# Four lanes sorted by expert and four dense, instead of five and three, with other planner costs, in a two-layer decoder

## The chip, the cores and the metric

The kernel runs on one core of one Trainium2 chip. The metric is the device time of one execution in microseconds. A run gives one such time; where a profile is shown, it is of one execution, and its span is the time from the first to the last instruction of the program.

## The reference, cut to what matters

The input `x` is 16 sequences of 128 tokens with 256 features, in float32. Two decoder layers are applied to it; every line of the sketch below adds its result to `x`, after a layer norm.

```python
x = x + attn0(ln(x))              # one head, causal, q k^T through one 256x256 matrix
x = x + xattn0(ln(x), ctx, mask)  # 16 heads of 16, keys and values from ctx
x = x + ffn0(ln(x))               # 16 blocks of 64, each token takes the best 4 by a router
x = x + attn1(ln(x))              # 16 heads of 16, own residual inside
x = x + xattn1(ln(x), ctx, cell)  # windows of 64, rotary, masked by cell, norms with gains
x = x + moe1(ln(x))               # 8 experts of 128 (SwiGLU), best 2 of a sigmoid router,
                                  # weights normalised and times 2.5, plus a shared expert of 256
```

The change is in how `moe1` is computed for some of the sequences, and in the order of everything.

## The kernel before

**Lanes and layers.** Two sequences form a lane (256 tokens), so there are eight lanes, 0 to 7. A lane's `x` stays in SBUF as a tile of 128 partitions by 2 by 256. Each lane goes through `layer_0` (causal attention, attention to the context, block FFN) and `layer_1` (self-attention, windowed attention to the context, and then the experts).

**Two ways through the experts.** A *dense* lane runs `expert_ffn` (L1272): all eight experts and the shared one are computed for all of its tokens (`gu` is gate and up, ten tiles of four matmuls; `y` is down, with 20 matmuls over two sequences), and a matmul with the router's weights (`wb`) scales each expert's `hm`. A *sorted* lane belongs to a group (`GROUPS`, L34). `routing` (L981) ranks the experts, counts the rows of each and scatters each token's normalised row into the DRAM buffer `to_experts`, four indirect DMAs of 128 rows for a lane. When the last lane of the group has been routed, `sorted_experts` (L1338) runs `plan` (L1075), which works out for each tile of 128 rows which expert it belongs to, and then all its `expert_tile`s (L1118): a gather of the expert's weights (`we<-in_L_experts`), a gather of the rows (`we<-to_experts`), two transposes (`xgt`), `gu<-we`, a transpose `hT`, `y<-we`, and a store to the DRAM buffer `by_experts`. A group of n lanes has 2 x n x 256 / 128 + 7 tiles, 27 for five lanes. The shared expert of a sorted lane runs by itself (`shared`, L1040). Then `combining` (L1168) gathers the results of each lane (`yg`, four gathers) and adds them to `x` with the token's weights, and the lane is written out. All indirect DMAs are issued from POOL's queue; loads, stores of `x`, and the swaps of the rotary step go through SP's queue; the stores to `by_experts` through ACT's.

**The order is made by a planner at build time.** The class `Turns` (L82) runs the lanes as threads. A thread says which engine it wants next and which buffers it takes; `run` (L229) picks the thread with the smallest key and records its next piece, so that the order on each engine's queue is fixed when the kernel is built. The planner has a clock of its own: `charge` adds a cost to an engine, `HOP` and `HOP_FROM_PE` stand for the way from one engine to another, `SWITCH` for a change of TensorE's array shape, `PART` for a piece on TensorE, `RELEASE` for the time until a buffer that was given back can be taken, `indexed` (L162) for an indirect DMA and its landing. `LIMITS` (L385) says how many buffers there are of each kind. `first` marks a thread in the midst of an attention's scores; the planner lets it go `LEAD` ns ahead of others. These numbers issue nothing; they only move the order.

**Lanes in flight.** `more` (L1447) starts the next (layer, lane) pair of `TURN` when fewer than `IN_FLIGHT` of them are under way (L1441). The dense `expert_ffn` of lanes that are not in a group starts when its weights (`late_weights`, L1408) have been loaded, one lane after another.

Of the kernel before, what the change touches and what calls it, by code (L numbers as in the profile page):

```python
# [30 lines left out]
BPC = P // 64  # L31
NE, TOPE = 8, 2

GROUPS = ((0, 1, 2, 3, 4),)  # L34


OUT = -(2.0**100)
# [44 lines left out]
class Turns:  # L82
# [3 lines left out]

    LEAD = 100.0
    HOP = 70.0  # L90
    HOP_FROM_PE = 200.0
    SWITCH = 91.0
    PART = 20.0
    RELEASE = 30.0

    def __init__(self, nc, limits):
        self.nc = nc
# [19 lines left out]
    def give(self, tag, n=1):  # L117
        self.tiles[tag] += [self.now.at + self.RELEASE] * n

    def shaped(self, shape):  # L120

        if shape != self.shape:
            self.shape = shape
            self.charge(PE, self.SWITCH)

# [36 lines left out]
    def indexed(self, out, out_index, src, src_index):  # L162

        at = lambda i: None if i is None else bass.IndirectOffsetOnAxis(ap=i, axis=0)
        self.charge(POOL, 1050.0)
        self.moved(4 * int(np.prod((src if src_index is None else out).shape)))
        self.now.at += 2000.0
        self.nc.gpsimd.indirect_dma_start(out, at(out_index), src, at(src_index))  # L168

    def fetch(self, out, src):  # L170
# [58 lines left out]
    def run(self, more):  # L229

        while True:
            more()
            best = None
            for i, th in enumerate(self.threads):
                if th.ask is None:
                    continue
                engine, takes = th.ask
                at = self.reach(th, engine)
                ok = True
                for tag, n in takes.items():  # L240
                    left = sorted(self.tiles[tag])
                    if not n:
                        continue
                    if len(left) < n:
                        ok = False
                        break
                    at = max(at, left[n - 1])
                first = th.holds or "s" in takes
                tiled = engine == PE and self.shape != WHOLE and ("s" in takes or "oT" in takes)
                key = (max(at - self.LEAD * first, self.free_at[engine] - first), not first, not tiled, th.rank, i)  # L250
                if ok and (best is None or key < best[0]):
                    best = key, th, at
            if best is None:
                assert not self.threads, "no thread can go on"
                return
            _, th, at = best
            engine, takes = th.ask
            for tag, n in takes.items():
                self.tiles[tag].sort()
                del self.tiles[tag][:n]  # L260
            th.at, th.last = max(th.at, at), engine
            if engine == PE:
                self.free_at[PE] += self.PART
            self.resume(th, None)
# [10 lines left out]
def decoder(ctx: ExitStack, tc: tile.TileContext, a: dict, out: bass.AP):  # L275
# [31 lines left out]
    first = wts.tile([P, 4, DC, D], F32, tag="f3", name="first")  # L307
# [51 lines left out]
    class Sorted:  # L359
# [16 lines left out]

    groups = [Sorted(k, lanes) for k, lanes in enumerate(GROUPS)]
    group_of = {l: g for g in groups for l in g.lanes}
# [4 lines left out]


    LIMITS = dict(  # L385
        bank=4, s=2, oT=1, xn=5, xT=4, qk=5, qs=3, kb=3, v=3, p=6, oS=2, on=4, xe=3, hm=5, tmp=3,
        rank=2, selT=2, p0=2, pT0=2, unseen=4, chosen=3, swap=1, words=1, top=3,
    )
    q = Turns(nc, LIMITS)

    def new(tag, shape, name, dtype=F32):
        return work.tile(shape, dtype, tag=tag, name=name, bufs=LIMITS[tag])
# [682 lines left out]
    def plan(g):  # L1075


        yield DVE, dict(tmp=3)
        T, E1 = g.tiles, NE - 1
        n_full = g.cap // P  # L1080
        little = lambda name, n: small.tile([P, n], F32, tag=name, name=name, bufs=1)
        n = little("n_of", NE)
        q.dve("tensor_tensor", n, g.next_row, g.first_row, ALU.subtract)
        q.dve("tensor_scalar", n, n, 1.0 / P, None, ALU.mult)
        t = new("tmp", [P, NE, n_full], "n_full")
        full = consts[:, C_IOTA : C_IOTA + n_full].unsqueeze(1).to_broadcast([P, NE, n_full])
        q.dve("tensor_tensor", t, along(n, n_full), full, ALU.is_gt)
        tiles = little("tiles", NE)
        q.dve("tensor_reduce", tiles, t, AX.X, ALU.add)
        tri = consts[:, C_TRI8 : C_TRI8 + NE * NE].rearrange("p (e f) -> p e f", f=NE)  # L1090
        t = small.tile([P, NE, NE], F32, tag="n_tri", name="n_tri", bufs=1)
        q.dve("tensor_tensor", t, tri, tiles.unsqueeze(1).to_broadcast([P, NE, NE]), ALU.mult)
        first = little("first", NE)
        q.dve("tensor_reduce", first, t, AX.X, ALU.add)
        q.dve("scalar_tensor_tensor", g.offset, first, float(P), g.first_row, ALU.mult, ALU.subtract)
        end = little("end", NE)
        q.dve("tensor_tensor", end, first, tiles, ALU.add)
        iota = consts[:, C_IOTA : C_IOTA + T]
        each = lambda v: v[:, 0:E1].unsqueeze(1).to_broadcast([P, T, E1])
        past = new("tmp", [P, T, E1], "past")  # L1100
        q.dve("tensor_tensor", past, along(iota, E1), each(end), ALU.is_ge)
        e = little("e_of", T)
        q.dve("tensor_reduce", e, past, AX.X, ALU.add)
        t = new("tmp", [P, T, E1], "t_of")
        q.dve("tensor_tensor", t, past, each(tiles), ALU.mult)
        f = little("f_of", T)
        q.dve("tensor_reduce", f, t, AX.X, ALU.add)
        q.dve("tensor_tensor", f, iota, f, ALU.subtract)
        q.dve("tensor_scalar", f, f, float(P), float(g.cap - P), ALU.mult, ALU.min)
        q.dve("scalar_tensor_tensor", f, e, float(g.cap), f, ALU.mult, ALU.add)  # L1110
        for to, v in ((g.tile_rows, f), (g.tile_weights, e)):
            if v is e:
                q.dve("tensor_scalar", v, v, float(P), None, ALU.mult)
            q.dve("tensor_scalar", v, v, consts[:, C_ROW : C_ROW + 1], None, ALU.add)
            q.dve("tensor_copy", to, v)
        q.give("tmp", 3)

    def expert_tile(g, i):  # L1118

        yield POOL, dict(p=1)  # L1120

        we = new("p", [P, HC, S], "we").rearrange("p h s -> p (h s)")
        xg = yo = we[:, 3 * D :]
        q.indexed(we[:, 0 : 3 * D], None, a["L1_experts"], g.tile_weights[:, i : i + 1])
        yield POOL
        q.indexed(xg, None, g.to_experts, g.tile_rows[:, i : i + 1])
        yield PE, dict(bank=1)
        t = bank([P, DC, S], "xgt")
        for d in range(DC):
            q.transpose(t[:, d, :], xg[:, d * P : (d + 1) * P], ident)  # L1130
        yield ACT, dict(xe=1)
        xgT = new("xe", [P, DC, S], "xgT")
        q.act("copy", xgT, t)
        q.give("bank")
        yield PE, dict(bank=1, tmp=1)
        gu = bank([P, 2, P], "gu2")
        for d in range(DC):
            wt = we[:, d * D : (d + 1) * D].rearrange("p (n f) -> p n f", f=P)
            q.matmul(gu, xgT[:, d, :], wt, start=d == 0, stop=d == DC - 1)
        q.give("xe")  # L1140
        yield ACT
        sg = new("tmp", [P, P], "sg2")
        q.act("activation", sg, gu[:, 0, :], AF.Tanh, scale=0.5)
        yield DVE, dict(p0=1)
        h = new("p0", [P, P], "h2")
        q.dve("scalar_tensor_tensor", sg, sg, 1.0, gu[:, 0, :], ALU.add, ALU.mult)
        q.dve("scalar_tensor_tensor", h, sg, 0.5, gu[:, 1, :], ALU.mult, ALU.mult)
        q.give("tmp")
        q.give("bank")
        yield PE, dict(bank=1)  # L1150
        t = bank([P, P], "hT2")
        q.transpose(t, h, ident)
        q.give("p0")
        yield ACT, dict(pT0=1)
        hT = new("pT0", [P, P], "hT")
        q.act("copy", hT, t)
        q.give("bank")
        yield PE, dict(bank=1)
        y = bank([P, D], "y2")
        q.matmul(y, hT, we[:, DC * D : 3 * D], start=True, stop=True)  # L1160
        q.give("pT0")
        yield ACT
        q.act("copy", yo, y)
        q.give("bank")
        q.load(g.by_experts[i * P : (i + 1) * P, :], yo, engine=ACT)
        q.give("p")
# [170 lines left out]

    def sorted_experts(g):  # L1338
        yield from plan(g)
        yield [expert_tile(g, i) for i in range(g.tiles)]  # L1340
        part_ended(g)

# [95 lines left out]
            if g.left == 0:  # L1438
                q.start(sorted_experts(g), 2 * NL + min(g.lanes), at)

    IN_FLIGHT = 6  # L1441

    TURN = [(0, l) for l in range(6)]
    for l in range(NL):
# [2 lines left out]
    def more():  # L1447
        n = begun[0]
        if n < IN_FLIGHT and n not in arrives:
            return  # L1450
# [123 lines left out]
```

## Time and profile before

| | us |
|---|---|
| median of three runs | 845.04 |
| lowest and highest | 844.15, 847.82 |
| the profiled execution | 846.62 |
| its span, first to last instruction | 844.8 |
| PE busy | 775.1 (92%), 7902 matmul records |
| DVE busy | 474.6 (56%) |
| ACT busy | 393.0 (47%) |
| POOL busy | 445.4 (53%) |
| PE's share of the chain that ended last | 72% |
| mean granted TensorE clock | 0.969 |

PE is TensorE's matmuls and PEld its weight loads, which lie beside them; DVE is VectorE, ACT ScalarE, POOL GpSimd, SP the queue of SyncE. A float32 matmul that is not a transpose leaves two records. Matmuls are pipelined, so their durations overlap, and the time that one costs is read from the distance between starts. In names of tiles the buffer numbers are left out. A line is mostly that of a helper (L135 the matmuls, L140 the transposes, L144 DVE, L149 ACT, L155 POOL, L168 the indirect DMAs), so groups are told apart by their tiles.

### The profile page before, as it was taken

How to read it: one execution, taken by the hardware profiler on the slowest of the kernel's cores; microseconds unless marked ns; L12 is line 12 of the kernel's file. 1: busy time of each engine (PE TensorE's matmuls, PEld its weight loads, DVE VectorE, ACT ScalarE, POOL GpSimd, SP SyncE). 2: the span in 40 equal slices, each digit the busy share in tenths (PEclk: the TensorE clock that was granted, in tenths of full speed). 3: DMA queues.
4: the chain of work that ended last, by engine and by line, in shares of the span. 5: the costliest groups of instructions: out<-in, count | busy, mean ns of one | idle time of the engine just before them, and what ended most of it. 6: DMA issues, size and time to landing. Idle time of an engine off the chain costs nothing.

```text
span 844.8 us, 19702 instructions
## 1 busy us (share of the span) xinstructions
PE 775.1 (92%) x7902; PEld 610.1 (72%) x7902; DVE 474.6 (56%) x1201; ACT 393.0 (47%) x874; POOL 445.4 (53%) x688
## 2 busy tenths in 40 slices
PE   6999999999999999999999899989894899988848
PEld 5877777887787876777687677757673577866726
DVE  5455746536654375827817768685667435245533
ACT  4545652533635565555465666547442344233100
POOL 5345654433533474728954678676646735450530
PEclk9999999999999999999999999989897899999969
DMA  9356642231110120001014111110205334551330
GB/s 306 99 158 191 192 118 69 80 103 26 28 38 24 34 77 2 28 26 51 13 65 151 46 45 45 45 38 33 64 33 150 113 101 137 156 181 48 103 94 25
DMA packets 60938, 70.43 MB, mean 83 GB/s; under 512 B 8848, under 2 KB 52496, under 8 KB 60208
## 3 DMA queue, kind: packets, MB, share of 16 engines
q1 hardware_dynamic: 51584, 46.24, 17.7%
q0 software_dynamic: 5376, 19.40, 7.7%
q10 hardware_dynamic: 3888, 3.54, 1.2%
q8 instruction: 62, 1.02, 0.5%
q14 instruction: 28, 0.23, 0.1%
HBM read 43.99 MB, written 20.97 MB: 77 GB/s over the span
## 4 chain that ended last, share of the span: by engine, by line
PE 72%; DVE 10%; POOL 7%; issue 4%; ACT 3%; DMA 2%; another core or an unknown queue 1%; SPq 0%; ACTq 0%; POOLq 0%; DVEq 0%
PE s L135 14%; PE pj L135 11%; PE y L135 9%; PE gu L135 9%; PE pr L135 8%; PE hp L135 7%; PE oT L135 4%; PE tps L140 3%; PE o L140 2%; DVE top L144 2%; POOL rstd L155 2%; POOL we L168 1%; ACT p L149 1%; POOL kb L155 1%
## 5 line engine op out<-in xcount | busy, mean ns | idle before, releaser
L144 DVE TENSOR_REDUCE top<-s 128x8 f32<-128x1024 f32 x96 | 112.8, 1217 | 49.6 <-PE s L135 49.0
L149 ACT ACTIVATE p<-s 128x1024 f32<-128x1024 f32 x96 | 93.2, 1022 | 48.6 <-PE s L135 45.4
L155 POOL TENSOR_TENSOR qs<-qT,less 128x512 f32<-128x512 f32 x48 | 61.4, 1281 | 58.0 <-ACT less L149 57.1
L155 POOL TENSOR_SCALAR rstd<-mv 128x2 f32<-128x2 f32 x77 | 18.6, 242 | 105.2 <-DVE mv L144 97.5
L149 ACT ACTIVATE sg<-gu 128x256 f32<-128x256 f32 (+1 forms) x67 | 22.2, 340 | 98.5 <-PE gu L135 56.3
L135 PE MATMUL hp<-srcT,L_w 128*128 128x256 f32 x256 | 65.2, 384 | 0.0
L135 PE MATMUL s<-kb,qT 32*128 32x256 f32 x768 | 61.2, 407 | 4.0 <-DVE top L144 2.6
L135 PE MATMUL s<-qs,kb 32*128 32x128 f32 x1536 | 58.8, 283 | 4.2 <-DVE top L144 1.4
L135 PEld LDWEIGHTS s<-qs,kb 32*128 32x128 f32 x1536 | 48.9, 186 | 18.1 <-issue 9.3
L155 POOL TENSOR_TENSOR rstd<-rstd,power 128x2 f32<-128x2 f32 x77 | 55.8, 724 | 6.4
L155 POOL TENSOR_SCALAR kb<-kT,consts 128x256 f32<-128x256 f32 x96 | 54.8, 582 | 4.6 <-ACT kT L149 3.6
L135 PE MATMUL y<-L_w,hm 128*128 128x256 f32 x256 | 57.0, 381 | 0.0
L135 PE MATMUL gu<-srcT,gu 128*128 128x256 f32 x192 | 50.4, 414 | 6.2 <-issue 2.6
L135 PE MATMUL oT<-p,v 128*32 128x128 f32 x1536 | 53.3, 278 | 1.3 <-ACT oS L149 0.7
L144 DVE TENSOR_TENSOR x<-x,y 128x512 f32<-128x512 f32 x16 | 11.0, 684 | 76.7 <-PE y L135 76.7
L135 PEld LDWEIGHTS s<-kb,qT 32*128 32x128 f32 x768 | 38.0, 186 | 21.5 <-issue 7.9
L135 PEld LDWEIGHTS y<-L_w,hm 128*128 128x128 f32 x256 | 48.2, 190 | 7.0 <-issue 0.5
L135 PEld LDWEIGHTS hp<-srcT,L_w 128*128 128x128 f32 x256 | 44.5, 191 | 9.8 <-issue 1.7
L135 PEld LDWEIGHTS gu<-srcT,gu 128*128 128x128 f32 x192 | 38.2, 207 | 16.4 <-issue 3.1
L144 DVE SCALAR_TENSOR_TENSOR sg<-sg,gu 128x256 f32<-128x256 f32 (+1 forms) x67 | 24.4, 364 | 44.9 <-ACT sg L149 41.6
L168 POOL DMA_INDIRECT we<-in_L_experts,tile_weights x27 | 26.4, 978 | 43.5 <-ACT hT L149 7.6
L135 PEld LDWEIGHTS oT<-p,v 128*32 128x32 f32 x1536 | 40.0, 111 | 12.9 <-issue 8.9
(216 smaller groups left out, 1791.3 us busy)
## 6 DMA issues: line engine op xcount, KB each, us to landing
to_experts<-zero SPq DMA_DIRECT2D x7, 1280.0 KB
unseen<-hidden SPq DMA_DIRECT2D x128, 64.0 KB
c<-in_ctx SPq DMA_DIRECT2D x16, 256.0 KB
by_experts<-we ACTq DMA_DIRECT2D x27, 128.0 KB
x<-in_x SPq DMA_DIRECT2D x8, 256.0 KB
L_w<-in_L_w SPq DMA_DIRECT2D x2, 1024.0 KB
hidden<-plain SPq DMA_DIRECT2D x32, 64.0 KB
swap<-kT SPq DMA_DIRECT2D x16, 128.0 KB
```

The source lines that it names most:

```text
L135: self.nc.tensor.matmul(out, lhsT, rhs, **kw)
L140: self.nc.tensor.transpose(out, src, ident)
L144: getattr(self.nc.vector, name)(out, *args, **kw)
L149: getattr(self.nc.scalar, name)(out, *args, **kw)
L155: getattr(self.nc.gpsimd, name)(out, *args, **kw)
L168: self.nc.gpsimd.indirect_dma_start(out, at(out_index), src, at(src_index))
```

## The change

The group has lanes 0 to 3, and lane 4 becomes dense; 27 expert tiles become 23, 20 scatters and 20 gathers of results become 16 each. In the planner, `LEAD` goes away and a thread in an attention is preferred only among equals, `SWITCH` is larger, `RELEASE` is zero, an indirect DMA lands 1.5 us later, and the expert tiles begin 3 us after the plan. There is one `xn` buffer more and one `qs` buffer less, and five (layer, lane) pairs are in flight instead of six.

```diff
-GROUPS = ((0, 1, 2, 3, 4),)
+GROUPS = ((0, 1, 2, 3),)
...
-    LEAD = 100.0
     HOP = 70.0
     HOP_FROM_PE = 200.0
-    SWITCH = 91.0
+    SWITCH = 115.0
     PART = 20.0
-    RELEASE = 30.0
+    RELEASE = 0.0
...
         self.moved(4 * int(np.prod((src if src_index is None else out).shape)))
-        self.now.at += 2000.0
+        self.now.at += 3500.0
         self.nc.gpsimd.indirect_dma_start(out, at(out_index), src, at(src_index))
...
-                first = th.holds or "s" in takes
                 tiled = engine == PE and self.shape != WHOLE and ("s" in takes or "oT" in takes)
-                key = (max(at - self.LEAD * first, self.free_at[engine] - first), not first, not tiled, th.rank, i)
+                key = (at, not (th.holds or "s" in takes), not tiled, th.rank, i)
...
-        bank=4, s=2, oT=1, xn=5, xT=4, qk=5, qs=3, kb=3, v=3, p=6, oS=2, on=4, xe=3, hm=5, tmp=3,
+        bank=4, s=2, oT=1, xn=6, xT=4, qk=5, qs=2, kb=3, v=3, p=6, oS=2, on=4, xe=3, hm=5, tmp=3,
...
     def sorted_experts(g):
         yield from plan(g)
+        q.now.at += 3000.0
         yield [expert_tile(g, i) for i in range(g.tiles)]
         part_ended(g)
...
-    IN_FLIGHT = 6
+    IN_FLIGHT = 5
```

## The prediction

> **What bounds the kernel now.** I read the table of windows first, then the timelines of the engines in the two windows that stand out. In the table each row is a stretch of the span (its bounds and length in us), the busy time of PE, PEld, DVE, ACT and POOL with the number of instructions, the granted TensorE clock, the DMA share and GB/s.
>
> ```profile
> 300.00:575.00 275.00, 260.29 (x3290) 200.06 (x3288) 181.84 (x435) 156.30 (x315) 185.36 (x289) 0.98 0.14 46
> 575.00:625.00 50.00, 45.41 (x553) 34.73 (x541) 34.72 (x91) 25.91 (x56) 29.47 (x46) 0.93 0.14 44
> 625.00:675.00 50.00, 34.95 (x323) 24.95 (x316) 26.26 (x71) 17.66 (x44) 33.51 (x45) 0.83 0.41 119
> 675.00:737.00 62.00, 59.85 (x429) 48.88 (x428) 25.75 (x78) 26.34 (x74) 29.90 (x37) 1.00 0.45 135
> 800.00:825.00 25.00, 11.78 (x37) 8.73 (x38) 10.60 (x27) 2.02 (x6) 9.05 (x10) 0.73 0.32 98
> ```
>
> TensorE sets the time: it is busy 92% of the span, and in 675:737, where a dense lane and expert tiles run together, it is idle 2.15 us of 62. It has two holes: 625:675 (idle 15.05 us, clock 0.83) and 800:825 (idle 13.22 us, clock 0.73). The change pays TensorE work for a chance to fill these two.
>
> In the first hole only lanes 6 and 7 are still in attention, no dense lane has begun, and lane 7's keys and queries have to be rotated and spread on POOL. POOL's timeline (start, length, instruction, idle before and its releaser):
>
> ```profile
> 633.11 1.28 POOL L155 TENSOR_TENSOR qT<-qT,consts 128x512 f32<-128x512 f32 x1 [3.49 <-DMA swap<-qT]
> 639.83 1.03 POOL L168 DMA_INDIRECT we<-in_L_experts,tile_weights  x1 [5.44 <-DVE on L144]
> 643.38 1.27 POOL L155 TENSOR_TENSOR qT<-qT,swap 128x512 f32<-128x512 f32 x1
> 652.75 1.28 POOL L155 TENSOR_TENSOR kT<-kT,consts 128x512 f32<-128x512 f32 x1
> 656.87 2.17 POOL L155 TENSOR_SCALAR kb<-kT,consts 128x256 f32<-128x256 f32 x4
> ```
>
> The first gather of weights waits 5.44 us, and the second half of qT's rotation stands behind it and two more; eight gathers (0.95 us and 0.30 between) lie between 639.83 and kT's first product at 652.75. TensorE meanwhile has only the first expert tiles.
>
> The second hole lies at the burst of 20 gathers (`yg`, 786.9 to 811.8, one every 1.25 us) that fetch the sorted lanes' results. ACT, DVE, POOL and PE in that place:
>
> ```profile
> 801.78 0.38 ACT L149 ACTIVATE sg<-gu 128x256 f32<-128x256 f32 x1 [15.16 <-remote]
> 815.08 0.94 ACT L149 ACTIVATE sg<-gu 128x256 f32<-128x256 f32 x3 [12.92 <-remote]
> 815.11 0.42 DVE L144 TENSOR_TENSOR hm<-wb,hm 128x256 f32<-128x256 f32 x1 [11.65 <-remote]
> 810.84 0.95 POOL L168 DMA_INDIRECT yg<-by_experts,results  x1 [0.30 <-issue]
> 815.59 0.37 PE L135 MATMUL wb<-selT,experts 128*128 128x256 bf16 x1 [10.47 <-DVE hm L144]
> ```
>
> The last dense lane's `gu` matmuls had been issued by 805.1, yet ACT and DVE get on only at 815.1, 3.3 us after the burst's last issue ended (811.79). What holds them is not named ("remote"); that it ends with the burst is what I build on. Then TensorE runs at half clock (0.50 in 815:820, 0.60 in 820:825).
>
> **Part 1: one lane goes from sorted to dense (+14.7 us of TensorE work).** Spacing in the last dense lane, where nothing waits:
>
> ```profile
> 826.43 1.89 PE L135 MATMUL gu<-srcT,gu 128*128 128x256 f32 x8
> 828.16 0.27 PE L135 MATMUL wb<-selT,experts 128*128 128x256 bf16 x1
> 828.27 1.89 PE L135 MATMUL gu<-srcT,L_shared 128*128 128x256 f32 x8
> 831.95 3.62 PE L135 MATMUL y<-down,hm 128*128 128x256 f32 x16
> 835.40 1.03 PE L135 MATMUL y<-L_shared,hm 128*128 128x256 f32 x4
> ```
>
> From start to start, eight `gu` take 1.73 us, one `wb` 0.11, sixteen `y` 3.45. A dense lane adds 8 experts x 1.73 = 13.8, 32 `y<-down` = 6.9, 8 `wb` = 0.9 and two `ptt` = 0.1: 21.7 us. The shared expert and the router are in both paths. The sorted path loses four expert tiles (27 become 23), each 0.86 for `gu<-we`, 0.22 for `xgt`, 0.11 for `hT`, 0.43 for `y<-we` by the spacing at 741 to 744: 6.5; and four transposes and five rank counts, 0.6. Net 21.7 - 7.1 = +14.6; two more changes of array shape in the order (333 to 335) at 0.09 each (eight `pj` take 1.73 or 1.82) make it +14.7. All of it is on the path, since TensorE is the bound.
>
> The other engines: DVE gets 8 `hm<-wb`, 8 `hm<-sg` and 8 `sg` at 0.42 and loses 4 x (2 x 0.29 + 0.48) plus small ones, about +6 us. ACT gains 8 x 0.38 and loses 4 x (0.37 + 0.37 + 0.27 + 0.27): -2 us. POOL loses 8 weight and token gathers, 4 scatters and 4 result gathers, 16 x 1.25 = 20 us. DVE is at 56% and hidden by TensorE; were it not, its 6 us would add.
>
> **Part 2: the first hole (-14 us).** In the new order the first weight gathers stand ahead of lane 6's last attention instead of in lane 7's rotation, and lane 4, now dense, has its `gu` between lane 7's swap of kT and the first scores that need it: 17.7 us of TensorE work there by the spacings above, against 7.0 before. The path it must cover is the swap's DMA (2.72), 1.28, 0.68, 1.27 and 2.17 for `kb`: 8.1 us. So 7.0 did not cover, and 17.7 covers it with some gathers in front. I let the stage become like its neighbour 575:625, idle 4.6 of 50: -10.5. A clock of 0.83 is 17 us at half, 0.93 is 7 us; ten us less at half, busy 70% of it, save another 3.5. Together -14.0. Bounds: -19 (all of the idle and 4 us of clock) and -2 (POOL queues as before; lane 7 late again).
>
> **Part 3: the burst (-7 us).** Sixteen gathers instead of 20 end it 4 x 1.25 = 5.0 us earlier, and a dense lane is again the work beside it: `gu` of four tiles, then blocked banks. Half of the 3.9 us that the slow clock cost on 7.8 busy us of 815:825 may go: -2. Behind it there is now a whole further dense lane, so nothing of the sorted path can end last. Bounds: 0 (same stall) and -16 (no stall).
>
> The Trainium skill, "TensorE: Matmul & The Clock Gate", the two states, speaks against the -2: the clock falls to half after an idle window of about 3.4 us, and a stall of 10.5 - 5.0 = 5.5 us is still longer. By it the term would be -5 and the time 840.7; the trace agrees in that 10.47 us of idle was followed by 0.50. The skill's "SBUF — State Buffer", who interferes with whom, says that a DMA never contends with a compute engine, which speaks against the burst as the cause; by it Part 3 is 0 and the time 845.7. The 15.16 and 12.92 us of ACT beside the burst decide against that page for me, but nothing here shows the mechanism.
>
> **Part 4: the planner's costs and limits (0, between -8 and +17).** LEAD, RELEASE, SWITCH and the later landing of gathers issue nothing; they move the order everywhere. The landing was 3.07 us for `yg` (794.41 to 797.48), so a longer assumption puts consumers further behind, which costs nothing where a dense lane fills. A third `qs` buffer less can hold back POOL's 1.28 us `qs`; it is written and read within one attention, and `xn` gets one more: 0. The 3 us from the plan keep the first gather from standing in POOL's queue with normalisations behind it: the 5.44 us above, already in Part 2. Five lanes in flight instead of six is the risk, priced below.
>
> **Sum.** 844.8 + 14.7 - 14.0 - 7.0 + 0 = 838.5 of span. The profiled execution is 846.6, 1.8 more than its span, and 1.6 above the median of 845.0; so 838.5 + 1.8 - 1.6 = **838.7 us**. A measurement of this kernel can tell about 0.5% (4.2 us) from no change: faster is below 840.8, slower above 849.3.
>
> **Rivals.**
> - **Five lanes starve the middle (slower).** With six lanes TensorE idles 14.7 us of 275 (5.3%) in 300:575; with two lanes left, 15.05 of 50 (30%). Straight between them, one lane fewer costs 6.2% of 275 = +17 us: 855.7. It makes the change slower from +10.6 us on. For it: DVE and POOL are at two thirds in that stretch, so waits are already near. Against: TensorE is busy 94.7% there, so six lanes are more than enough in most of it, and a straight line overstates the loss of one. Chance 0.2.
> - **The first hole is not filled.** POOL's queue delays lane 7 as before, Part 2 gives -2 and Part 3 -3: 844.8 + 14.7 - 5 = 854.5, so 854.7. Chance 0.15.
> - **Half of the gain.** Parts 2 and 3 bring 10 to 18 together: 841 to 849. Chance 0.2.
> - **Both holes go.** -19 and -14: 826.5, so 826.7. For it: three dense lanes stand behind the sorted tiles. Chance 0.13.
>
> **How the numbers follow.** The forecast (830 to 840.8) has 0.32, and with both holes gone (below 830) 0.45 are faster, 0.2 the same, 0.35 slower. 825 to 858 leaves out about a tenth at each end; the forecast's own range is 830 to 841.
>
> **What would show it.** Right: 256 records of `gu<-srcT,gu` and 128 of `y<-down`, no window of 50 us between 550 and 700 with TensorE below 43, and a stall beside `yg` of 4 to 7 us. Wrong: idle in 300:575 above 25 us (five lanes); a hole with `kb` late on POOL; a stall at `yg` as long as before with 16 gathers, or none, which would take the burst's length out as its measure.

## Result: 1.1% slower, and the profile after

The changed kernel takes 854.36 us (median of four runs, 853.54 to 856.78) where the kernel before took 845.34 beside it (844.15 to 847.82): a ratio of 1.0108, 95% interval 1.0076 to 1.0139. The forecast of 838.7 has the wrong sign. The profiled execution has a span of 855.0 us against 844.8, and the mean granted clock rose from 0.969 to 0.982.

The table of windows of the changed kernel (columns as before: bounds, length, busy time of PE, PEld, DVE, ACT, POOL, granted clock, DMA share, GB/s):

```profile
300.00:575.00 275.00, 259.81 (x3133) 200.04 (x3125) 180.14 (x421) 151.75 (x313) 179.01 (x278) 0.99 0.14 46
575.00:625.00 50.00, 39.89 (x598) 28.41 (x598) 34.97 (x82) 26.40 (x50) 27.95 (x41) 0.95 0.12 39
625.00:675.00 50.00, 42.33 (x284) 33.29 (x288) 29.29 (x81) 21.49 (x58) 27.68 (x41) 0.91 0.34 106
675.00:737.00 62.00, 57.32 (x566) 44.57 (x567) 26.97 (x74) 26.94 (x69) 33.79 (x46) 1.00 0.34 107
...
800.00:855.00 55.00, 49.31 (x223) 40.97 (x223) 25.17 (x64) 6.67 (x18) 1.38 (x2) 0.96 0.09 30
```

The deep hole of before (34.95 busy of 50 in 625:675) is now spread: 39.89 and 42.33 in two neighbours that together were 80.36 and are 82.22. The stretch from 800 on is full but for its first us and the 3.9 us behind TensorE's end. And 300:575 looks the same, 259.81 against 260.29. By busy time alone one would say that the change gained. Busy time misleads here, because a matmul that follows its neighbour late, or runs at half clock, is busy too.

So I split TensorE's time in another way, my own working from the starts of its records. Each record is given the distance it keeps to its neighbour where nothing waits at full clock (0.216 us for a float32 matmul of 256 columns, as in Part 1, and so on for each kind). Their sum is TensorE's **own work**. What its span up to its last record has beyond that is **lost**: idle, half clock, late neighbours. The last column is the time from TensorE's end to the end of the span.

| | own work | lost in the first 400 us of own work | lost from 400 to 600 | lost in the rest | behind TensorE | span |
|---|---|---|---|---|---|---|
| before | 709.3 | 38.4 | 60.4 | 32.8 | 4.1 | 844.8 |
| after | 724.0 | 52.9 | 52.9 | 21.4 | 3.9 | 855.0 |

The work grew by 14.7 us, exactly what Part 1 says. The end became better by 11.4, the middle by 7.5, and the first part became worse by 14.5. The first part ends at about 440 us before and 457 after; the first sorted lanes have scattered their rows by then (from 375 and 377 us on), but no gather and no expert tile of the group has begun. For that last figure the prediction had only its Part 4, at 0.

At the burst, ACT, PE and POOL of the changed kernel (start, length, instruction, idle before and releaser):

```profile
799.18 0.38 ACT L148 ACTIVATE sg<-gu 128x256 f32<-128x256 f32 x1 [7.39 <-remote]
804.12 0.66 ACT L148 ACTIVATE sg<-gu 128x256 f32<-128x256 f32 x2 [4.55 <-remote]
800.53 3.78 PE L134 MATMUL gu<-srcT,gu 128*128 128x256 f32 x8 [6.17 <-DVE sg L143]
804.63 1.99 PE L134 MATMUL gu<-srcT,gu 128*128 128x256 f32 x8 [0.32 <-DVE hm L143]
800.54 1.15 POOL L167 DMA_INDIRECT yg<-by_experts,results  x1 [0.30 <-issue]
```

TensorE's stall is 6.17 us where it was 10.47, and the eight `gu` after it take 3.78 us where the next eight take 1.99: half clock, as before (the granted clock is 0.56 in 800:805 and 1.00 behind it). Behind the stall a whole dense lane follows with almost nothing lost. The Trainium skill, "TensorE: Matmul & The Clock Gate" (what's actually happening), puts the fall to half clock after about 3.4 us of idle; 6.17 us followed by half speed agrees with it.

### The profile page after: what moved, and what is told of

Its sections match the earlier page's. It is cut to its first block, busy times and chain, and to the rows that moved or that the text cites. A ratio compares the mean times of both kernels' runs of the same rounds, so it can differ in the third digit from the quotient of the medians.

```text
span 855.0 us, 19810 instructions
## 1 busy us (share of the span) xinstructions
PE 790.5 (92%) x7963; PEld 621.8 (73%) x7963; DVE 482.3 (56%) x1201; ACT 391.8 (46%) x865; POOL 427.3 (50%) x668
## 4 chain that ended last, share of the span: by engine, by line
PE 74%; DVE 14%; ACT 4%; issue 3%; POOL 2%; another core or an unknown queue 1%; DMA 1%; POOLq 0%; DVEq 0%; ACTq 0%
PE s L134 14%; PE y L134 12%; PE gu L134 11%; PE pj L134 10%; PE pr L134 8%; PE hp L134 6%; DVE top L143 4%; PE oT L134 4%; PE tps L139 2%; ACT p L148 2%; PE o L139 2%; DVE xn L143 1%; POOL rstd L154 1%; DVE st L143 1%
## 5 line engine op out<-in xcount | busy, mean ns | idle before, releaser
L148 ACT ACTIVATE sg<-gu 128x256 f32<-128x256 f32 (+1 forms) x71 | 24.6, 349 | 105.3 <-PE gu L134 85.2
L134 PE MATMUL gu<-srcT,gu 128*128 128x256 f32 x256 | 63.7, 400 | 8.1 <-DVE sg L143 6.2
L134 PE MATMUL s<-kb,qT 32*128 32x256 f32 x768 | 63.6, 407 | 4.8 <-ACT p L148 3.6
L134 PEld LDWEIGHTS s<-qs,kb 32*128 32x128 f32 x1536 | 48.6, 186 | 19.9 <-issue 10.0
L134 PEld LDWEIGHTS gu<-srcT,gu 128*128 128x128 f32 x256 | 49.0, 199 | 18.7 <-DVE sg L143 6.4
L154 POOL TENSOR_TENSOR rstd<-rstd,power 128x2 f32<-128x2 f32 x76 | 55.3, 727 | 6.3
L154 POOL TENSOR_SCALAR kb<-kT,consts 128x256 f32<-128x256 f32 x96 | 52.7, 560 | 3.6 <-ACT kT L148 2.8
L148 ACT ACTIVATE hm<-hp,cols 128x256 f32<-128x256 f32 x64 | 26.8, 470 | 45.3 <-PE hp L134 44.8
L148 ACT COPY oS<-oT 128x512 f32<-128x512 f32 x48 | 28.3, 590 | 39.1 <-PE oT L134 35.7
```

Of the source, the lines that this page charges most:

```text
L134: self.nc.tensor.matmul(out, lhsT, rhs, **kw)
L148: getattr(self.nc.scalar, name)(out, *args, **kw)
L154: getattr(self.nc.gpsimd, name)(out, *args, **kw)
```

## Experiments

Eighteen kernels ran. In the code, "before" and "after" name the kernel that was edited. Ratios are to the kernel before, run beside it on the same chip; its medians there were 845.9 to 848.2. Where two kernels did not run side by side, the text gives the difference of their ratios and that of their medians, since the kernel before itself moves by up to 2.9 us from one set of runs to another.

### The group, and the lanes in flight

**g4_six**: before with the group of four. With RELEASE at 20 as well, since the planner finds no order otherwise.

```diff
-GROUPS = ((0, 1, 2, 3, 4),)
+GROUPS = ((0, 1, 2, 3),)
-    RELEASE = 30.0
+    RELEASE = 20.0
```

> The kernel before with lanes 0 to 3 sorted and lane 4 dense, and nothing else of the change: six pairs in flight, the planner's costs as before but RELEASE 20 for 30 (30 gives no order that can be built with four lanes). Theory 'five in flight' (the 16 us that TensorE loses more up to the end of layer 0 come from five lanes instead of six, and four sorted lanes by themselves gain): 845 + 14.7 of work - about 20 of idle after layer 0 = 840, and TensorE's lost time up to the last block FFN stays near 38 us as before. Rival 'the dense lane' (the extra work is what is lost, the rest comes out even): 855 to 860. Rival 'every new order' (the order of a planner scatters by that much whatever is changed): anything from 840 to 865, with lost time up to the last block FFN anywhere from 38 to 55.

867.87 us, ratio 1.0225 (1.0174 to 1.0276).

**before_release20**: the same RELEASE alone, the control.

> The kernel before with RELEASE 20 for 30 and nothing else, a number that issues nothing and moves the order from TensorE's 285th row on. It is the partner of the run with lanes 0 to 3 sorted, six in flight and RELEASE 20. Theory 'every new order' (the order before is a picked one, and any other loses ten us and more): 855 to 870, TensorE's lost time up to the last block FFN 45 or more where before has 38. Rival 'four sorted lanes do it' (with six in flight the dense lane disturbs the middle): 845 to 849, lost time near 38.

849.14, ratio 1.0036 (1.0007 to 1.0065). The control costs 2 to 3 us, so the group of four with six in flight costs 16 to 17: its 14.7 of work, and 66.1 us lost in the first 400 of own work where the control loses 42.1, against gains behind it.

**g5_five**: before with five in flight (LEAD is 90 because 100 gave no order).

```diff
-    LEAD = 100.0
+    LEAD = 90.0
-    IN_FLIGHT = 6
+    IN_FLIGHT = 5
```

> The kernel before with five pairs in flight instead of six and LEAD 90 for 100 (100 gives no order that can be built), still five lanes sorted. Theory 'five in flight': 845 + 16 = 861, the loss lying ahead of the last block FFN. Rival 'the dense lane': 845, within 3. Rival 'every new order': 840 to 865.

879.75, ratio 1.0372 (1.0355 to 1.0389). It loses 63.9 us in the first 400 of own work. Taken by itself this is the rival of the five lanes, nearly twice as dear as I had priced it; what LEAD 90 has in it was not run alone.

**g4_five**: both, and nothing else of the change.

```diff
-GROUPS = ((0, 1, 2, 3, 4),)
+GROUPS = ((0, 1, 2, 3),)
-    IN_FLIGHT = 6
+    IN_FLIGHT = 5
```

> The kernel before with two parts of the change: a group of four lanes and five lanes in flight; the planner's settings as before. Theory 'the group of four pays for itself only where the planner leaves the sorted lanes' end uncovered or the early order poor': the group of five with five in flight lost 164.7 us on TensorE (879.4 of span); work rises by 14.7, and with three dense lanes as cover the losses of 16.7 at the end go: 870 to 885. Rival 'five in flight needs the fourth dense lane, and the two belong together' (as after's settings suggest): 850 to 862, near after's 854.

845.71, ratio 0.9977 (0.9957 to 0.9996). Both of my expectations were wrong. Each part alone, with the nudge of RELEASE or LEAD that it needed, costs 16 to 32 us, and together they cost nothing: 32.3 us lost in the first 400 of own work, less than before's 38.4. So neither five lanes nor the group has a price of its own there; what has one is the order that the planner finds for them. This run is also the base for all that follows: the same own work as the changed kernel (724.0) and the same five lanes in flight, in 9 to 11 us less.

**after_g5**: the changed kernel with the group of five.

```diff
-GROUPS = ((0, 1, 2, 3),)
+GROUPS = ((0, 1, 2, 3, 4),)
```

> The changed kernel with five lanes sorted again and everything else of the change kept. Theory 'five in flight': 854.4 - 14.7 of work + about 20 that the dense lane fills after layer 0 = 860. Rival 'the dense lane': 845 or less. Rival 'every new order': 840 to 865.

873.88, ratio 1.0296 (1.0272 to 1.032). Less work by 14.7 and yet 16 to 20 us slower than the changed kernel, which none of the three expected; 25.9 us lie behind TensorE's end, where the changed kernel has 3.9. TensorE's last matmuls and POOL's last gather:

```profile
847.80 1.03 PE L134 MATMUL y<-L_shared,hm 128*128 128x256 f32 x4
860.19 0.95 POOL L167 DMA_INDIRECT yg<-by_experts,results  x1 [0.30 <-issue]
```

The dense lanes are done while the sorted lanes' results are still being gathered. The group of four pays here because one more dense lane covers that end.

**after_six** and **after_six_then_five**: the changed kernel with six in flight (SWITCH is 95, as 115 gave no order), and with six for the first ten starts only.

```diff
-    IN_FLIGHT = 5
+    IN_FLIGHT = 6
```

> The changed kernel with six pairs in flight instead of five and SWITCH 95 for 115 (115 gives no order that can be built). Theory 'five in flight': 854.4 - 16 = 838, with TensorE's lost time up to the last block FFN back near 38 us. Rival 'the dense lane': 854, within 3. Rival 'every new order': 840 to 865, and the lost time ahead of the last block FFN does not go with the number in flight.

> The changed kernel with six pairs in flight for the first ten starts and five from then on. Theory 'five in flight': the lost time up to the last block FFN falls from 54 to about 40 and the rest stays, 840 to 845. Rival 'every new order': 855 to 870.

862.32 (1.0155, 1.0123 to 1.0187) and 869.43 (1.0257, 1.0236 to 1.0278): the theory of the five lanes had expected 838 and 840 to 845, and is refuted by both. With six throughout, the first 400 us of own work lose 44.8 in place of 52.9, and the rest gives back more (91.4 in place of 74.3); with six for the first ten, the first part loses 63.6. But SWITCH differs in the first of them, so the next run belongs beside it.

**after_switch100**: the changed kernel with SWITCH 100 in place of 115.

> The changed kernel with SWITCH 100 for 115, which issues nothing and moves the order from TensorE's 676th row on. Theory 'every new order': 862 to 875, that is, the changed kernel's order is a picked one too. Rival 'the number in flight sets the middle': 854, within 3, and lost time up to the last block FFN within 3 us of the changed kernel's 54.

862.33, ratio 1.0149 (1.0089 to 1.0208; 855.11 to 865.75). Against the changed kernel's 1.0108 (1.0076 to 1.0139) that is 3 to 8 us more, by ratios or by medians, and the intervals overlap. A number that issues nothing and leaves the work alone does as much as six lanes with SWITCH 95. So the difference of after_six cannot be put down to the lanes.

### The landing part

**before_landing**: before with the two edits that make gathers land later in the planner.

```diff
-        self.now.at += 2000.0
+        self.now.at += 3500.0
         self.nc.gpsimd.indirect_dma_start(out, at(out_index), src, at(src_index))
...
         yield from plan(g)
+        q.now.at += 3000.0
```

> The kernel before with the gather part of the change alone: an indirect DMA lands 1.5 us later in the planner and the tiles begin 3 us after the plan. The order is the same up to TensorE's row 1636 of 3130. If the distance from the plan helps the hole behind the plan, TensorE loses 5 to 10 us less between the first gather of weights and the first dense gu, 836 to 842. If any new order costs, 850 to 865, with the loss in the part that is reordered only.

854.72, ratio 1.0081 (1.0061 to 1.0101). TensorE itself loses 116.8 us, 14.7 less than before, but its last matmul ends at 826.0 and the sorted lanes go on for 27.7 us. So the time lies where 'any new order' had put it, but the loss does not: TensorE gained, and the end was left uncovered. The ends of PE, of POOL's gathers and of DVE's combine:

```profile
825.03 1.03 PE L135 MATMUL y<-L_shared,hm 128*128 128x256 f32 x4
844.24 0.95 POOL L168 DMA_INDIRECT yg<-by_experts,results  x1 [0.30 <-issue]
847.23 0.48 DVE L144 SCALAR_TENSOR_TENSOR x<-yg,weight,x 128x256 f32<-128x256 f32 x1 [0.41 <-DMA yg<-by_experts,results]
```

**landing_held_lane**: the same, and the last dense lane starts only when all expert tiles are done, to cover that end.

```diff
-        if ready and experts_begun[0] < len(dense):
+        if ready and experts_begun[0] < len(dense) and (experts_begun[0] < 2 or tiles_left[0] <= 0):
```

> The kernel before with the landing part alone (3.5 us for gathers, 3 us from the plan), and the last dense lane starts in the order only when all 27 expert tiles are done. Theory 'the landing order loses least on TensorE, and only its uncovered end costs': the landing kernel's last matmul ended at 826.0 and its gathers 27.7 us later; with a whole dense lane (about 27 us of work) behind the last tile the end is covered, the burst stalls that lane by about 10 us as before, and the last tiles, with no dense lane between them, lose 3 to 6 us: 826 + 4 + 10 + 4 = 840 to 848 of span less the gain of the freed banks; under 845 if the theory holds. Rival 'the tiles need the dense lanes between them': the last ten tiles wait on their chain (gather, transpose, copy, activation, transpose, copy), TensorE loses 15 us or more there and the time is 850 or more.

876.65, ratio 1.0355 (1.0308 to 1.0401): my expectation of 840 to 848 was wrong, and so was the rival's reason. The tiles are not what starves TensorE. The held lane itself is:

```profile
807.76 0.47 PE L140 MATMUL hT<-consts,h 128*128 128x128 f32 x1 [1.01 <-DVE h L144]
841.54 0.39 PE L135 MATMUL ptt<-ident,chosen 128*128 128x128 bf16 x2 [27.18 <-DVE chosen L144]
836.72 0.95 POOL L168 DMA_INDIRECT yg<-by_experts,results  x1 [0.30 <-issue]
838.65 0.29 DVE L144 TENSOR_REDUCE rank<-gt 128x16 f32<-128x128 bf16 x1 [4.49 <-POOL gt L155]
```

Its router's comparison (`gt`, on POOL) stands behind the 20 gathers, and its ranks on DVE behind the combines that follow each landing. TensorE waits 27.18 us. Here a dense lane could cover the burst only if its router were through POOL before the burst begins.

**after_no_landing**: the changed kernel without the landing part.

> The changed kernel without the landing part: gathers are taken to land after 2 us and the first tile stands at once behind the plan. If the landing part is what shortens the first hole and the tail here, TensorE waits for gathers again: 4 to 10 us more, 858 to 865. If it matters only where the end is uncovered (as with the kernel before), the work behind the last tile grows from 62 to 79 us of TensorE's own time and the time stays within 4 us of 854. If the early order is what costs, the stage before the first expert tile stays as it is (about 54 us lost to the last block of layer 0) in both.

852.5, ratio 1.0059 (1.0033 to 1.0085), 849.88 to 856.07: 2 to 5 us less than the changed kernel, by medians or beside their partners. In its order the own work behind the last tile is 79 us in place of 62, so the end is covered in both, and the landing part gains nothing there. Nor is it what costs: the first 400 us of own work lose 53.9 here.

### The burst

**before_half_burst**: before, with 10 of the 20 gathers of results left out and TensorE's order unchanged.

```diff
-            q.indexed(y[:, i, :], None, g.by_experts, by[:, i : i + 1])
+            if k == 0:
+                q.indexed(y[:, i, :], None, g.by_experts, by[:, i : i + 1])
+            else:                       # charged to the planner, not issued
...
-                x[l][:, j, :], y[:, i, :], ...
+                x[l][:, j, :], y[:, j * TOPE, :], ...
```

> The kernel before, with 10 of the 20 gathers of results left out; the planner is charged for them all the same, so that TensorE's order is the same instruction for instruction. The combine uses the first chosen expert's row in place of the second's: that part of the computation is changed. Theory 'the burst holds the engines': the stall of ACT and DVE beside the result gathers (12.92 and 11.65 us before) ends with the last gather plus some 3 us, so with a burst of 12.5 us in place of 25 it is gone or below 3 us; the time falls by 9 to 13 us, to about 834 to 838. Rival 'the dense lane's own chain' (the wait is something else that merely ends there): the stall stays at 10 us or more and the time stays within 3 us of before. Rival 'length only by half': a stall of 5 to 7 us and 839 to 841.

835.01, ratio 0.9851 (0.9799 to 0.9903): 13 us less, at the edge of what the first theory gives. ACT, POOL's last gather, and PE behind them:

```profile
803.96 0.94 ACT L149 ACTIVATE sg<-gu 128x256 f32<-128x256 f32 x3 [14.67 <-PE gu L135]
801.01 0.95 POOL L168 DMA_INDIRECT yg<-by_experts,results  x1 [0.31 <-issue]
805.30 1.99 PE L135 MATMUL gu<-srcT,gu 128*128 128x256 f32 x8 [2.22 <-DVE hm L144]
```

ACT still waits, 14.67 us, and is released 2.0 us after the last gather's issue ended (801.96). But this now comes at about the time when TensorE runs out of free banks, so TensorE idles 2.22 us in place of 10.47 and keeps its clock. The part of the loss behind 650 us of own work falls from 23.5 to 10.0 and nothing else moves. So with ten gathers fewer ACT is released 11.1 us earlier and TensorE's stall is shorter by 8.3 us: the length of the burst sets when the stall ends, and that is shown. That ACT's own wait would be gone or below 3 us was wrong: it did not shrink.

### Which of the planner's settings costs

Here all kernels have the group of four, five lanes in flight and 724.0 us of own work. "Costs" are LEAD gone from the key, SWITCH 115 and RELEASE 0; "limits" are `xn=6` and `qs=2`.

**g4_five_costs**: g4_five with the costs.

```diff
-    SWITCH = 91.0
+    SWITCH = 115.0
-    RELEASE = 30.0
+    RELEASE = 0.0
...
-                key = (max(at - self.LEAD * first, self.free_at[engine] - first), not first, not tiled, th.rank, i)
+                key = (at, not (th.holds or "s" in takes), not tiled, th.rank, i)
```

> Group of four, five in flight, and the planner's costs of the changed kernel (no LEAD in the key, SWITCH 115, RELEASE 0); limits and landing as before. Theory 'the costs spoil the early order': TensorE loses 50 us or more up to the last block of layer 0, as the changed kernel does (54.3), and the time is 852 to 857. Theory 'the limits (qs 2) spoil it': the early loss stays near 32 us and the time is 843 to 848.

864.49, ratio 1.0199 (1.0164 to 1.0235).

**after_limits_undone**: the changed kernel with `xn=5` and `qs=3`, that is g4_five with costs and landing.

> The changed kernel with the buffer limits of before (xn 5, qs 3). By 'the costs': 851 to 858, loss up to the last block of layer 0 still above 50 us. By 'the limits': back to 844 to 849, with an early loss of some 32 us.

879.45, ratio 1.0394 (1.0361 to 1.0428).

**g4_five_landing**: g4_five with the landing part.

> Group of four, five in flight, the landing part (3.5 us for gathers, 3 us from the plan), costs and limits as before. The early order comes before any gather, so its loss stays near 32 us. 43 us of TensorE's work stand behind the last tile, which covers the end (28 us). If landing later spares TensorE waits in the hole, as it did with five sorted lanes (14.7 us less), 830 to 842; if not, within 4 us of 845.7. Both theories of the early cost expect an early loss near 32 here.

846.5, ratio 0.9986 (0.9967 to 1.0004).

**g4_five_limits_landing**: g4_five with limits and landing part.

> Group of four, five in flight, the landing part and the limits xn 6, qs 2, costs as before: the changed kernel without its planner costs. By 'the costs': early loss near 32 us and a time of 835 to 848, like the run with the landing alone. By 'the limits': early loss of 50 or more and 852 to 858.

858.12, ratio 1.0128 (1.0088 to 1.0167).

| costs | limits | landing | kernel | median | lost first 400 | 400 to 600 | rest |
|---|---|---|---|---|---|---|---|
| | | | g4_five | 845.71 | 32.3 | 62.1 | 20.1 |
| | | x | g4_five_landing | 846.50 | 33.4 | 50.5 | 31.4 |
| x | | | g4_five_costs | 864.49 | 57.0 | 55.3 | 23.0 |
| x | | x | after_limits_undone | 879.45 | 52.9 | 56.7 | 35.4 |
| | x | x | g4_five_limits_landing | 858.12 | 54.2 | 48.6 | 27.1 |
| x | x | | after_no_landing | 852.50 | 53.9 | 51.9 | 16.6 |
| x | x | x | after | 854.36 | 52.9 | 52.9 | 21.4 |

Either the costs or the limits are enough to spoil the first part of the order (53 to 57 us lost in place of 32 to 33), and the two do not add. I had expected one of them to be it alone. Each setting gives one order, and the cost belongs to that order: a number nearby gives another one, as SWITCH 100 and RELEASE 20 show. The windows show it ahead of any gather and expert tile: 300:400 of g4_five, g4_five_costs, g4_five_limits_landing and the changed kernel, one line from each:

```profile
300.00:400.00 100.00, 99.44 (x1359) 76.84 (x1358) 61.11 (x136) 55.85 (x114) 65.23 (x94) 1.00 0.08 26
```

```profile
300.00:400.00 100.00, 94.32 (x1292) 71.32 (x1294) 63.32 (x144) 54.82 (x112) 61.53 (x93) 1.00 0.09 28
```

```profile
300.00:400.00 100.00, 93.36 (x1173) 70.66 (x1175) 54.34 (x129) 49.99 (x101) 58.32 (x94) 0.95 0.08 25
```

```profile
300.00:400.00 100.00, 94.50 (x1277) 71.81 (x1273) 62.59 (x143) 54.61 (x112) 59.81 (x91) 0.98 0.09 27
```

TensorE idles 0.6 us of 100 in the first and 5 to 7 in the others. No single wait carries it. What PE waited for in 170:460 of g4_five_costs (total, times, longest), and then in the changed kernel:

```profile
PE n L135 <- DVE on L144: 5.5, 1, 5.5
PE s L135 <- ACT p L149: 2.3, 4, 1.1
PE oT L135 <- ACT oT L149: 1.6, 1, 1.6
```

```profile
PE o L139 <- ACT oS L148: 2.3, 2, 1.6
PE s L134 <- ACT p L148: 2.3, 4, 1.1
PE gu L134 <- DVE sc L143: 1.5, 1, 1.5
```

All such waits in that window sum to 5.3 us in g4_five, 17.5 with the costs, 13.4 with limits and landing, and 12.2 in the changed kernel: many short waits, most of them of attention steps. The waits account for 7 to 12 us of what is lost more; the rest is half clock and late neighbours. That their predecessors stand too close in front in the order is how I read it, and was not tested. Which of the three costs does it (the key, SWITCH, RELEASE), and which of the two limits, was not tried one by one.

### A version that beats both

**g4_five_distance** has, of the landing part, only the 3 us behind the plan; **g4_five_landing_only** only the 3.5 us of landing.

```diff
         yield from plan(g)
+        q.now.at += 3000.0
```

> Group of four, five in flight, only the 3 us from the plan; gathers land after 2 us in the planner, costs and limits as before. 64 us of TensorE's work stand behind the last tile (73 without the 3 us, 43 with the whole landing part), so the end is covered. If the wait of 5.5 us for qs and those around the plan in the hole come from gathers standing ahead in POOL's queue, the distance takes them away: 835 to 842, which beats both kernels. If not: 844 to 849, as the two neighbours.

> Group of four, five in flight, only the landing of gathers after 3.5 us. 50 us of TensorE's work stand behind the last tile, and the burst of 16 gathers (20 us) and the 28 us that an end took after its start are just covered: lost at the end below 3 us, where the whole landing part lost 10.3. If the landing brings the gain ahead of the last score: 836 to 842. If the two halves only work together: 844 to 850.

843.37 (ratio 0.9954, 0.9936 to 0.9973) and 844.69 (0.9974, 0.9952 to 0.9996; its runs reach from 838.59 to 847.95). The first is faster than both kernels of the case, by half a per cent over before and 1.3 to 1.5% over the changed one; beside g4_five (0.9977, 0.9957 to 0.9996) its gain is not clear of the noise. It lies between the two times that I had given, 835 to 842 and 844 to 849, and whether it was the wait for `qs` that shrank is not shown: from 500 to 550 us of own work it loses 5 to 8 us less than g4_five, and behind 650 some 4 us more.

## Why the prediction was wrong, step by step

- **Part 1 (+14.7) was right**: own work 709.3 to 724.0, with 256 records of `gu<-srcT,gu` and 128 of `y<-down`.
- **Part 2 (-14) had the right mechanism and was twice too large.** From the last matmul of layer 0's block FFN to the last attention score, TensorE lost 59.1 before and 51.7 after: -7.4, inside the bounds of -19 and -2. The two stages are parted by the last score, at 695 us before and 713 after, so how the gain is split between this part and the next is rough. It is the cover that came true, and not a free queue on POOL. In the changed kernel, lane 6's `kb` and the first gather, and then, around lane 7's `kb`, a gather, lane 4's `gu` and the first scores that need it:

```profile
620.81 2.44 POOL L154 TENSOR_SCALAR kb<-kT,consts 128x256 f32<-128x256 f32 x4
628.34 1.10 POOL L167 DMA_INDIRECT we<-in_L_experts,tile_weights  x1 [0.16 <-issue]
674.30 1.00 POOL L167 DMA_INDIRECT we<-in_L_experts,tile_weights  x1 [4.21 <-DVE sg L143]
676.71 2.17 POOL L154 TENSOR_SCALAR kb<-kT,consts 128x256 f32<-128x256 f32 x4
682.01 1.99 PE L134 MATMUL gu<-srcT,gu 128*128 128x256 f32 x8
685.66 1.15 PE L134 MATMUL s<-kb,qT 32*128 32x256 f32 x16
```

  Lane 6's rotation is now through before the gathers begin. Lane 7's rotation still stands behind a gather that waits 4.21 us, and its `kb` comes at 676.71, 20 us later than in the kernel before (656.87). TensorE loses little by it, since lane 4's `gu` and the expert tiles lie in front of the scores, as the prediction had it.

  And a window of 50 us at 38.30 busy (600:650) remains, below the 43 that I had set: the neighbour stage got worse while the hole got better, and I had let the neighbour stand.
- **Part 3 (-7) was too small**: from the last attention score to TensorE's end it lost 34.0 before and 21.2 after, -12.8, inside the bounds of -16 and 0. The stall of 6.17 us is in the 4 to 7 that I gave. Taking away half of the burst in the kernel before gave -13 too. The clock did fall to half again, as the skill's rule had it against my -2, so the gain is in the stall (4.3 us shorter, where the sum had 5.0) and in what follows it. The other rule that I weighed, that a DMA does not contend with a compute engine ("SBUF — State Buffer", who interferes with whom), isn't refuted: the run shows that the burst's length sets when the stall ends, but not what holds TensorE's results until then (last section).
- **Part 4 (0) is the step that failed.** I argued that numbers that issue nothing only move the order, and so priced them at nothing. Of the 10.2 us by which the span grew, Part 1 is 14.7, Part 2 -7.4 and Part 3 -12.8; the 15.7 that are left lie up to the last matmul of layer 0's block FFN, where TensorE lost 38.5 before and 54.3 after. Against g4_five, which has the group, the five lanes and none of the planner's settings, the changed kernel is 9 to 11 us slower (854.36 to 845.71; ratios 1.0108 to 0.9977), with 20.6 more lost in the first 400 us of own work and 9.2 less in the next 200. I had bounded Part 4 by -8 and +17, and took the value of no effect between them for want of a row, though that is no likelier than either side. I looked for its cost in the buffers' waits on POOL, and it came mostly in attention steps between PE, ACT and DVE, before the first gather.
- Parts 1 to 3 sum to -6.3 in the prediction. g4_five, the nearest kernel to them alone, has a span of 842.5, -2.3: right in sign, and less than can be told from no change.
- **The rival of the five lanes had the right size (855.7) for a wrong reason.** Its mark was idle of over 25 us in 300:575; there are 15.2, as before (14.7). And with the planner's settings of before, five lanes and four sorted lose less in the first part than six did. **The rival of the unfilled hole (854.7)** also lands on the number and is wrong as well: the hole and the burst brought 20.2 us together, more than the 10 to 18 of "half of the gain".

## What to carry to other kernels

A planner's cost, a buffer limit or a number of threads in flight had no sign of its own here: with the same group and the same five lanes in flight, ten settings lie between 843 and 879 us, and a nudge of one number (SWITCH 115 to 100, RELEASE 30 to 20) moves 2 to 8 us. Give such an edit the spread of its neighbours as its range, look for its cost in stages that the change does not mention, and try the parts that change work apart from those that only change order. A transfer at the end is covered by work only if that work needs nothing from the queue that issues the transfer.

## What the runs showed of the hardware

- **Beside a burst of gathers ACT and DVE wait, and get on only when it is over.** ACT was released 3.3 us after the last gather's issue ended in the kernel before, 2.0 with half of the burst, 2.4 in the changed kernel, and 3.1 in g4_five, where it waited 14.01 us. There TensorE idled only 4.7 us, in three pieces of 1.14 to 1.88, since it had 40 `y` matmuls with nothing to wait for; its granted clock still was 0.55 in 780:785:

```profile
775.78 1.31 PE L135 MATMUL y<-L_shared,hm 128*128 128x256 f32 x4
778.73 0.22 PE L135 MATMUL ptt<-ident,chosen 128*128 128x128 bf16 x1 [1.64 <-issue]
783.91 0.37 ACT L149 CAST selT<-ptt 128x256 bf16<-128x256 f32 x1 [14.01 <-remote]
```

  Most of these rows name the releaser only "remote". The trace's records of the semaphores say more: these instructions wait for the count that finished matmuls raise, not for a gather's landing, and it is TensorE's count that comes late. In the kernel before, matmuls that by their records ended between 798.57 and 805.12 raised it at 815.05 to 815.27, 10.2 to 16.5 us later; in the changed kernel those that ended between 794.14 and 794.36 raised it at 804.10 to 804.16, some 9.9 us later. The median over the whole run is 0.015 us. Since the ends of matmuls are modelled, the trace doesn't tell whether the matmuls were late or only their signal, and why the burst should hold either stays open.
- **A sorted end that nothing covers costs 26 to 28 us** behind TensorE's last matmul (25.9 and 27.7 in two kernels): 20 gathers, one every 1.25 us, and a combine of 0.48 us that follows each landing.
